# The thirteenth kernel column of a depthwise convolution as sixteen 32x32 products, two channel groups at a time

## The chip, the cores and the metric

The kernel runs on one NeuronCore of a Trainium2 chip. Its engines are TensorE (PE in the profile, with its weight loads as PEld), VectorE (DVE), ScalarE (ACT), GpSimd (POOL) and SyncE (SP). SP, ACT and POOL issue the transfers; 16 DMA engines carry them out. The metric is the time of the device in microseconds (us), as the median of three runs.

## The reference, cut to what matters

The network has four layers on an image batch x of shape (8, 384, 32, 32). Layers 0 and 1 are state space blocks; the change touches only one step of their preparation work. Layers 2 and 3 are what the change is about:

```
# layer 2: one 13x13 depthwise convolution and six smaller ones, each with a
# batch norm; the kernel folds all seven into one 13x13 kernel per channel
out = bn0(dwconv(x, w_lk)) + sum(bn_j(dwconv(x, w_bj, dilation r_j)))
# layer 3: a pointwise product, then again a 13x13 depthwise convolution
x_pw = bn(einsum('bchw,oc->bohw', x, pw_w)) + x
out  = gelu(bn(dwconv(x_pw, dwk_w)) + bn(x_pw * dw1_w))
```

So there are two 13x13 depthwise convolutions over 384 channels, 8 images and 32x32 pixels, with a pointwise product (384 to 384 channels) between them. All numbers are fp32.

## The kernel before, in words

The function `network` runs the two state space layers first (`layers`, some 6,340 us of the span), then the first depthwise convolution (`conv.run`, writing x4), the pointwise product (`point.run`, writing x5), and the second depthwise convolution (writing the output). The class `Depthwise` does both convolutions.

**One group.** A group is eight channels; `N2` is 48 groups. An image tile `xp` has 128 partitions: four blocks of 32 image rows, of which block s holds the rows shifted by s columns. A weight tile `wt` holds, for each of the 8 channels, a 128 x 32 matrix for each j in 0..3 (`KP` = 4). One product of `wt[:, c, :, j]` (128 x 32) with the image at column offset 4j (128 x 256: 8 images of 32 columns) sums over all kernel rows and over the four kernel columns 4j to 4j+3. Four channels q go to the four 32-partition quarters of one PSUM tile `ps`, so a set is 16 products (L1008), and a group has two sets a. 13 columns need four steps j, and three of the 16 columns of the last step are zeros (`prepare`, L208 to L210, lays them out so). In the profile every fp32 product is two matmul instructions with a weight load each: 48 x 32 x 2 = 3,072 for one convolution, 6,144 for both.

**Filling an image tile.** `images` (L976 to L984) has POOL issue two transfers for a group; they fill one of the four blocks for each half of the channels. Then DVE makes the shifted blocks by four copies: two of 32 x 1212 elements (L999, one for each half h) and two of 64 x 1208 (L1000 and L1001). The last of these, L1001, reads blocks 2 and 3 of the second half and so follows the second L999. There are `NB` = 4 image tiles, and the images of group g + 3 are issued in the turn of group g.

**Weights.** `kernels` (L967 to L970) loads a group's weights by four transfers of 128 KB, three issued by SP and one by ACT, in pieces of 512 bytes. There are `NK` = 11 weight tiles; the first ten groups of a convolution are loaded ahead by POOL (`early`), and the weights of group g + 10 are issued in the turn of group g, which has to wait until group g - 1 has left its tile.

**Eviction.** ACT evicts a set (`ACTIVATE`, L1013, 128 x 256) into a tile `o`, of which there are four, and then issues its store (L1014, 128 KB). The first convolution stores rows of 1,024 bytes, the second pieces of 128 bytes to the output. PSUM has eight banks; four hold `ps` tiles, and four are set aside by a placeholder, `past_ps`.

**Order.** An engine works through its instructions in one order, fixed when the program is built, by the order in the code and by what is ready. An instruction that waits holds up all behind it on its engine, and a DMA issue is such an instruction: ACT's evictions, ACT's stores and ACT's weight loads are one queue. The transfers of SP and ACT signal eight semaphores in turn (101 to 105, 107, 109 and 110 in the trace), so a new one waits until the transfer that used its semaphore last has landed. The image and weight tiles lie in SBUF behind a placeholder of `PAST` = 16,100 floats per partition, where the layers' tiles are still in use at their end; the tiles of the pointwise product lie behind them.

## Time and profile before

| what | us |
|---|---|
| median of three runs (lowest, highest) | 6903.32 (6903.21, 6914.22) |
| span of the profiled execution | 6870.5 |
| what lies around the span (median less span) | 32.8 |
| first convolution: first product to last eviction's start | 6349.3 to 6521.4 |
| pointwise product: first to last matmul | 6535.2 to 6660.8 |
| second convolution: first product to last eviction's start | 6671.5 to 6866.4 |

All positions are us from the start of the span. The clock granted to TensorE is full in both convolutions (PEclk 1.00 in all but their first microseconds). A "DMA share" above 1 means that the 16 engines had on average more than one packet each under way. The column "(x..)" counts instructions; of the 128 matmul instructions of two groups one can read how many pairs of groups went by in a stretch.

### The profile page before, as it was taken

What the parts mean: (1) busy time and instruction counts of PE and PEld (TensorE: products, weight loads), DVE (VectorE), ACT (ScalarE), POOL (GpSimd) and SP (SyncE); (2) the same over time, 40 slices, a digit from 0 to 9 for tenths busy, and PEclk for the clock granted to TensorE, in tenths of its full rate; (3) what the DMA queues carried; (4) which work ended last, traced back from release to release, by engine and by line L of the source; (5) the groups of instructions that cost most, each with busy time, mean ns of one, the idle gap of its engine ahead of it and who ended that gap; (6) DMA issues with size and microseconds to landing.
All of it is one profiled execution on the core that took longest, in us unless ns stands there. A gap on an engine that the chain in (4) does not pass through costs nothing. (4 is left out here: it accounts for less than half of the span.)

```text
span 6870.5 us, 76836 instructions
## 1 busy us (share of the span) xinstructions
PE 5851.1 (85%) x22562; PEld 2082.8 (30%) x22562; DVE 5755.9 (84%) x4598; ACT 4475.3 (65%) x7478; POOL 5285.7 (77%) x2858
## 2 busy tenths in 40 slices
PE   6787787888988888888888888888898888978988
PEld 2222222222322232222222232223232222323745
DVE  3899999899888888889889898888888898791837
ACT  4777666767676776867676767767676667653222
POOL 3889888888888888888898888888888788772412
PEclk7789988999999999999999999999999989989999
DMA  4565555665656666666756566666675655754979
GB/s 130 162 175 158 154 158 151 162 182 159 182 155 165 169 170 163 161 168 170 176 157 179 161 175 165 167 165 169 161 172 160 165 162 162 173 132 123 287 213 236
DMA packets 944578, 1160.04 MB, mean 169 GB/s; under 512 B 301264, under 2 KB 537344, under 8 KB 944160
## 3 DMA queue, kind: packets, MB, share of 16 engines
q1 hardware_dynamic: 782080, 1059.11, 59.0%
q10 hardware_dynamic: 146928, 51.02, 3.1%
q0 software_dynamic: 15152, 44.99, 2.3%
q8 instruction: 183, 3.00, 0.2%
q14 instruction: 235, 1.93, 0.1%
HBM read 904.67 MB, written 199.49 MB: 161 GB/s over the span
## 5 line engine op out<-in xcount | busy, mean ns | idle before, releaser
L532 POOL TENSOR_TENSOR dbu<-B,ru 128x1024 f32<-128x1024 f32 x1536 | 3583.2, 2357 | 168.7 <-DMA B<-bc 92.3
L525 ACT ACTIVATE h<-rd,A 128x512 f32<-128x512 f32 x3072 | 2117.4, 691 | 887.4 <-DVE hc L561 521.2
L553 DVE TENSOR_TENSOR_SCAN h<-h,state,dbu 128x512 f32<-128x512 f32 x1152 | 1482.5, 1287 | 210.5 <-ACT h L525 74.6
L561 DVE TENSOR_TENSOR hc<-h,C 128x1024 f32<-128x1024 f32 x1152 | 1411.0, 1225 | 139.8 <-DMA C<-bc 22.2
L556 DVE TENSOR_TENSOR_SCAN h<-h,dbu 128x1024 f32<-128x1024 f32 x576 | 1317.9, 2288 | 221.0 <-ACT h L525 149.9
L572 POOL TENSOR_TENSOR hc<-dbu,C 128x1024 f32<-128x1024 f32 x384 | 903.1, 2352 | 702.1 <-DVE dbu L556 358.5
L583 PE MATMUL acc<-hc,fold 128*32 128x512 f32 x6144 | 1158.0, 662 | 321.6 <-DVE hc L561 239.9
L415 PE MATMUL mm<-xt,wi 128*128 128x512 f32 x2232 | 1116.9, 638 | 57.2 <-ACT delta L491 18.9
L703 PE MATMUL f<-mx,wi 128*128 128x512 f32 x1116 | 589.0, 635 | 141.7 <-ACT fh L707 99.9
L415 PEld LDWEIGHTS mm<-xt,wi 128*128 128x128 f32 x2232 | 419.9, 201 | 754.5 <-issue 435.5
L604 PE MATMUL mm<-u,wo 128*128 128x512 f32 x1152 | 589.9, 653 | 63.4 <-DMA wo<-in_l_out_dram 51.6
L716 PE MATMUL f<-fh,wo 128*128 128x512 f32 x1128 | 573.1, 625 | 73.2 <-DMA wo<-in_fc_dram 64.1
L583 PEld LDWEIGHTS acc<-hc,fold 128*32 128x32 f32 x6144 | 164.6, 112 | 1132.3 <-DVE hc L561 513.3
L553 DVE TENSOR_TENSOR_SCAN dbu<-h,state,dbu 128x512 f32<-128x512 f32 x384 | 470.5, 1267 | 15.8 <-ACT h L525 8.0
L556 DVE TENSOR_TENSOR_SCAN dbu<-h,dbu 128x1024 f32<-128x1024 f32 x192 | 438.1, 2282 | 48.1 <-ACT h L525 47.3
L439 PE MATMUL mm<-xp,taps 128*64 128x512 f32 x1536 | 408.7, 654 | 21.2 <-ACT state L569 8.1
L984 POOL DMA_DIRECT2D xp<-x x192 | 124.3, 648 | 382.1 <-PE ps L1008 182.7
L305 ACT ACT_TABLE_LOAD x289 | 370.8, 1283 | 5.9 <-PEq L1214 0.7
L1008 PE MATMUL ps<-xp,wt 128*32 128x256 f32 x6144 | 343.8, 381 | 34.7 <-ACT o L1013 21.1
L604 PEld LDWEIGHTS mm<-u,wo 128*128 128x128 f32 x1152 | 229.8, 208 | 427.1 <-issue 355.6
L580 PE MATMUL acc<-u,skip 128*128 128x512 f32 x384 | 226.1, 673 | 153.2 <-DVE u L588 150.6
L425 ACT ACTIVATE xp<-mm,b_in 64x512 f32<-64x512 f32 x384 | 261.6, 681 | 143.1 <-PE mm L415 140.3
(168 smaller groups left out, 5726.4 us busy)
## 6 DMA issues: line engine op xcount, KB each, us to landing
ru<-uu SPq DMA_DIRECT2D x1536, 128.0 KB
rd<-dd SPq DMA_DIRECT2D x1536, 128.0 KB
wi<-w_in SPq DMA_DIRECT2D x372, 192.0 KB
xp<-xp SPq DMA_DIRECT2D x384, 128.5 KB
dd<-delta SPq DMA_DIRECT2D x192, 256.0 KB
uu<-delta SPq DMA_DIRECT2D x192, 256.0 KB
wo<-in_l_out_dram SPq DMA_DIRECT2D x96, 384.0 KB
wi<-fc_w SPq DMA_DIRECT2D x192, 192.0 KB
```

The costliest lines, as they stand in the source:

```text
L415: nc.tensor.matmul(s.ps[m], w[:, c], s.xt[:, c], start=c == 0, stop=c == KC - 1)
L439: nc.tensor.matmul(s.ps[d][64 * h : 64 * h + 64], taps[:, h, j], xp[h][:, 2 * j : 2 * j + T], start=j == 0, stop=j == 1,)
L525: nc.scalar.activation(y[:, q], s.dr[d][1][h][:, q], AF.Exp, scale=s.layer.A[:, at : at + 1])
L532: nc.gpsimd.tensor_tensor(dbu, s.B[g].unsqueeze(1).to_broadcast([P, 2, T]), s.ur[d][1][h], ALU.mult)
L553: nc.vector.tensor_tensor_scan(to[:, q], y[:, q], dbu[:, q], first, ALU.mult, ALU.add)
L556: nc.vector.tensor_tensor_scan(flat_to, flat_y, flat_b, first, ALU.mult, ALU.add)
L561: nc.vector.tensor_tensor(hc, to, s.C[g].unsqueeze(1).to_broadcast([P, 2, T]), ALU.mult)
L572: nc.gpsimd.tensor_tensor(hc, y, s.C[g].unsqueeze(1).to_broadcast([P, 2, T]), ALU.mult)
L583: nc.tensor.matmul(s.acc[d][32 * r : 32 * r + 32], k["fold"], tiles[r // 2][:, r % 2], start=False, stop=n == PER - 2)
L604: nc.tensor.matmul(s.ps[m], w[:, d], s.us[d], start=d == 0, stop=d == KD - 1)
L703: nc.tensor.matmul(s.ps[m], s.w["in", m][:, c], s.xt[:, c], start=c == 0, stop=c == KC - 1)
L716: nc.tensor.matmul(s.down, s.w["out", 2 * m + f // KD][:, f % KD], s.hs[f], start=f == 0, stop=f == KF - 1)
```

## The change

1. **Products.** Groups are taken in pairs, so a turn has four sets. Each set does only three steps j (12 columns of the kernel) with 128-row products. The 13th column is done at the end of the turn: for set k (0 to 3) its four products use only the 32 rows of block k, placed at rows 32k and columns 32q of the array. These are 16 products of 32 x 32 into four PSUM banks. `prepare` now puts the 13th column into all four blocks of the weight tile, with two DVE copies for each block in place of one.
2. **Copies.** The four copies of a group become a function `shifts`. Its last one (the old L1001) is done by ACT. It is called for the next pair, after this pair's products and ahead of this pair's evictions.
3. **Buffers.** Eight PSUM banks in place of four, six image tiles in place of four with images issued four or five groups ahead, nine groups of weights loaded early in place of ten.
4. **Memory.** The pools of the pointwise product are opened first, so that they lie in front; `PAST` falls to 3,200 floats, and `past_ps` goes.

```
-                n = (KS - s + 3) // 4
-                nc.vector.tensor_copy(rows[:, s, low : low + KS, 0:n], t[:, s::4].rearrange("p j r -> p r j"))
+                part = rows[:, s, low : low + KS]
+                nc.vector.tensor_copy(part[:, :, 0 : KP - 1], t[:, s : KS - 1 : 4].rearrange("p j r -> p r j"))
+                nc.vector.tensor_copy(part[:, :, KP - 1 :], t[:, KS - 1 :].rearrange("p j r -> p r j"))
...
-    NB, AHEAD = 4, 3
-    NK, EARLY = 11, 10
+    NB, AHEAD = 6, 4
+    NK, EARLY = 11, 9
...
+    def shifts(self, g):
+        nc, n, xp = self.nc, B * WIDE, self.xps[g % self.NB]
+        for h in range(2):
+            low, q = 2 * HW * h, slice(4 * h, 4 * h + 4)
+            nc.vector.tensor_copy(xp[low + HW : low + 2 * HW, q, 0 : n - 1], xp[low : low + HW, q, 1:n])
+        nc.vector.tensor_copy(xp[2 * HW :, 0:4, 0 : n - 2], xp[: 2 * HW, 0:4, 2:n])
+        nc.scalar.copy(xp[: 2 * HW, 4:8, 2:n], xp[2 * HW :, 4:8, 0 : n - 2])
...
+        for g in range(2):
+            self.shifts(g)
+        for pair in range(0, self.N2, 2):
+            sets = [(g, a) for g in (pair, pair + 1) for a in range(2)]
+            for g in (pair + self.AHEAD, pair + self.AHEAD + 1):
+                if g < self.N2:
+                    self.images(g, src)
+            for g in (pair + self.EARLY, pair + self.EARLY + 1):
+                if g < self.N2:
+                    self.kernels(g, table, (nc.sync, nc.scalar, nc.sync, nc.sync))
+            tops = []
+            for g, a in sets:
...
+                for j in range(KP - 1):
+                    x = columns(g, 0, P, 4 * j)
                     for q in range(4):
...
+            for k, (g, a) in enumerate(sets):
+                low, high = HW * k, HW * (k + 1)
+                x, wt = columns(g, low, high, KS - 1 - k), self.wts[g % self.NK]
+                for q in range(4):
+                    nc.tensor.matmul(
+                        tops[k][HW * q : HW * (q + 1), : B * HW], wt[low:high, 4 * a + q, :, KP - 1],
+                        x[:, 4 * a + q, :, 0:HW], start=False, stop=True, tile_position=(low, HW * q),
+                    )
+            for g in (pair + 2, pair + 3):
+                if g < self.N2:
+                    self.shifts(g)
+            for (g, a), ps in zip(sets, tops):
                 o = self.work.tile([P, B, HW], F32, tag="o", name="o")
                 nc.scalar.activation(o, ps[:, : B * HW], func, bias=bias[:, 2 * g + a : 2 * g + a + 1])
                 nc.scalar.dma_start(store(2 * g + a), o)
...
+        point = Pointwise(tc, st)
         past = st.enter_context(tc.tile_pool(name="past", bufs=1, reuse_waits="tile"))
         past.tile([P, PAST], F32, name="past")
-        past_ps = st.enter_context(tc.tile_pool(name="past_ps", bufs=1, space=PSUM, reuse_waits="tile"))
-        past_ps.tile([P, 4 * T], F32, name="past_ps")
         conv = Depthwise(tc, st)
         conv.early(got["k2"])
-        point = Pointwise(tc, st, conv.psum, a["pw"])
+        point.fill(conv.psum, a["pw"])
```

## The prediction

> **What bounds the kernel now.** I first read the busy times by stretch, to see who is full in the two convolutions.
>
> ```profile
> core 0: us, PE busy (x) PEld busy (x) DVE busy (x) ACT busy (x) POOL busy (x), PEclk, DMA share, GB/s
> 6349.00:6400.00 51.00, 50.68 (x940) 42.09 (x944) 49.02 (x61) 12.75 (x27) 16.82 (x29) 1.00 1.00 266
> 6400.00:6520.00 120.00, 117.07 (x2140) 83.71 (x2132) 104.88 (x131) 31.79 (x68) 48.25 (x75) 1.00 1.06 289
> ...
> 6700.00:6840.00 140.00, 122.40 (x2132) 79.70 (x2128) 105.83 (x135) 31.74 (x67) 45.22 (x67) 1.00 1.13 246
> ```
>
> A pair of groups is 128 matmul instructions, so a pair takes 51 x 128/940 = 6.95 us at the start of the first convolution, 120 x 128/2140 = 7.18 us in its rest, and 140 x 128/2132 = 8.40 us in the second. PE looks full, and DVE is close. But the DMA share is 1.06 and 1.13: a pair moves 16 transfers (8 of weights, 4 of images, 4 stores), and the engines that carry them never rest. Next, what PE's own speed would be: single starts in the trace come four within 39 ns, and the next four 216 ns later, so 128 instructions are 32 x 0.216 = 6.91 us. Only the first stretch runs at that. What holds the rest up is in the waits (total us, times, longest) of 6360 to 6520:
>
> ```profile
> ACT o L1013 <- PE ps L1008: 45.4, 28, 3.3
> ACT o L1013 <- DMA x<-o: 34.0, 30, 2.6
> ACT o L1013 <- DMA wt<-k_rows: 32.2, 21, 2.5
> ```
>
> and in the chain that ended last, from 6300 on:
>
> ```profile
> by line: DMA wt<-k_rows 22.8%; PE ps L1042 22.0%; DMA x<-o 9.2%; DMA out_dram<-o 9.0%; PE ps L1008 5.9%; issue 4.0%; ACTq L970 3.8%; ACTq L1014 3.8%; ACT o L1013 3.1%; PE f L716 2.8%; DVE xp L999 2.2%; DMA wo<-in_fc_dram 2.0%; DMA xt<-x 1.6
> ```
>
> The pointwise product (L1042) is bound by PE. In the convolutions the chain runs through transfers of some 5 us each and through ACT's issues; their products (L1008) are only 5.9%. A late eviction is mostly an ACT that stood before a DMA issue whose semaphore was not yet free. The weights show it too: early in the first convolution they are issued some 40 us ahead of their products, for group 40 only 9 us. So **the transfers, served through ACT's one queue, bound both convolutions** from about 6400 on.
>
> **Part by part.** *Products.* Each set loses one of four steps: per pair 12 steps of 2 x 0.216 = 5.18 us remain. The 16 small products (32 instructions) have no row. If all run abreast they cost one step, 0.43; if only the four columns run abreast, as now, 4 x 0.43 = 1.73; if one after another, 32 x 0.216 = 6.91. The trace does show what a change of shape costs: 522 ns from a 128x128 product of 512 columns to one of another shape, 429 between equal ones, so 0.09 us twice per pair. I take the first: 5.18 + 0.43 + 0.19 = 5.8 us, 1.1 us less per pair. Under a pace of 7.18 and 8.40 set by others this gain is not on the path, save at the start of a convolution.
>
> [...]
>
> *Copies.* DVE drops from four to three copies a group, 3 x 0.80 = 2.4 us for 3.2, no longer close to any bound. ACT gains one of 1208 elements per group. Its price from ACT rows:
>
> ```profile
> L456 ACT ACTIVATE zs<-zs 128x512 f32<-128x512 f32 x192 | 109.8, 619 | 0.7
> L569 ACT COPY state<-h 128x2 f32<-128x2 f32 x576 | 92.0, 160 | 331.6 <-DVE hc L561 324.2 <-DVE den L639 4.2
> L1013 ACT ACTIVATE o<-ps,b 128x256 f32<-128x256 f32 x192 | 91.0, 474 | 312.7 <-PE ps L1008 144.6 <-DMA wt<-k_rows 67.5 <-DMA x<-o 35.8
> L636 ACT ACTIVATE lg<-lg,top 8x1024 f32<-8x1024 f32 x8 | 9.2, 1148 | 0.2
> L151 ACT COPY b<-mm 128x96 f32<-128x96 f32 x2 | 0.5, 239 | 0.8 <-PE mm L150 0.8
> ```
>
> From 2 to 96 elements a copy grows by 0.84 ns each, so 0.160 + 1206 x 0.84 = 1.17 us; from 512 to 1024 the slope is 1.03, giving 1.34. I take 1.2, the copy's own rows: 2.4 us per pair.
>
> *ACT's queue.* Now ACT's own time per pair of the first convolution is 4 x 0.474 evicting, 4 x 0.36 and 2 x 0.37 issuing (median 0.33), some 0.2 between: 4.3 us. The DMA waits above are 66.2 us in 160 us, 22.3 pairs: 3.0 us each. With the copies its own time is 6.7 us. **The waits are the open price**: a landing that ACT awaits goes on while it copies, so up to 2.4 us could be absorbed; but the two weight issues now stand behind four stores in a burst, the eighth transfer before the second of them is one of these stores, and the copies and the next pair's evictions stand behind it. Waits all gone: the pace stays at the transfers' 7.18. All kept: 9.7. I take half, 6.7 + 1.5 = 8.2: +1.0 us for 24 pairs, **+24 us** (0 to +60).
>
> In the second convolution ACT's weight issue itself blocks, because the stores before it are 1,024 pieces of 128 bytes:
>
> ```profile
> L970 ACTq DMA_DIRECT2D wt<-k_rows x31: 1392/2099/3273, 6702.0 to 6829.3; - x31
> ```
>
> (min/median/max ns; 0.33 us in the first convolution.) Own time 1.9 + 4 x 0.41 + 2 x 0.33 + 0.2 + 2.4 = 6.8 us, and 2 x 1.77 = 3.5 of blocking. Half kept is 8.55: +0.15 for the 16.7 pairs of 6700 to 6840, and +1.2 for four pairs before, which ran at some 7.4: **+7 us**. All kept, 10.3: 1.9 x 16.7 + 2.9 x 4 = +43. None: 0.
>
> [...]
>
> *Ends.* A pair's four evictions now come together after its last product, where one was left: 3 x (0.47 + 0.36 + 0.1) = 2.8 us later at the end of each convolution, **+5.6 us** (0 to 7, if the last weights land earlier). *Start of a convolution.* Faster products pull stores forward while the DMA share is still 0.96 in 6671 to 6700: **-2 us** (-5 to 0).
>
> *Buffers.* Nine early weight groups with 11 tiles mean two groups loaded in the first turn in place of one: the same 11, the same bytes. The images one turn earlier move no byte less. Eight banks let PE run a pair further ahead of ACT; with ACT the slower, that fills up and then gives nothing (0). *Preparation.* 24 DVE copies of 128x39 and 128x52 (175 and 242 ns) become 24 of 39 and 24 of 13 elements: +1.4 us if the new ones cost as little as 60 ns (the smallest DVE row, a memset of one element), +3.8 at 160; DVE is 84% busy there, so I take **+2**. *Memory.* 12,768 floats of the pointwise pools plus 3,200 are 15,968, about the old 16,100, so the convolution's tiles come free as now. But three POOL memsets (1.6 us each) and SP's load of `pw` now wait for the layers' end; queued ahead of POOL's first image issue (6330.2), they would hold it until some 6347 + 4.8, and PE would start 9 us later; behind it, nothing. **+2** (0 to +9).
>
> *Sum* on the profile: 24 + 7 + 5.6 - 2 + 2 + 2 = 38.6; 6870.5 + 38.6 = 6909. With the 32.8 us between the span and the median: **6942 us**. With all waits gone, 0 + 0 + 5.6 - 2 + 2 + 0 gives 6909; with all kept and the late start 60 + 43 + 5.6 + 4 + 9 gives 7025.
>
> **Rivals.** *A, the transfers absorb it.* ACT's waits shrink as its work grows and the DMA share stays above 1: some +5 us, 6908. For it: the waits are for landings, which an occupied ACT need not see. Against: the burst of four stores.
>
> *B, faster.* The DMA engines are not at their limit, and a shorter PE turn pulls more through: the pace falls to ACT's own time, 6.7 us in the first convolution (-0.45 x 24 = -11) and 7.1 with a little blocking in the second (-1.3 x 20 = -26), with +5 at the ends: 6871. For it: within 6355 to 6357, single slices moved up to 386 GB/s. Against: 120 us at 289 with a share of 1.06. It decides once the stretches after 6400 move over some 300 GB/s, that is, a pair under 6.9 us.
>
> *C, the small products do not overlap.* PE needs 12.3 us a pair: (12.3 - 7.18) x 24 + (12.3 - 8.40) x 24 = +217, 7120. Four abreast would be 7.1 us, hidden under ACT. *The change does not do what it says* if ACT's copies end up behind the evictions in its order: then the shifts of the next pair come late, and PE waits where ACT does; this lies within the first case.
>
> **Chances.** ACT's queue 0.52, A 0.32, B 0.12, C 0.04. The range is 6888 to 7005: it leaves out most of B below, and above C and the all-kept end. A measurement of this kernel can tell about 0.2%, 14 us, from no change: same is 6889 to 6917, most of A and the small end of the first case, 0.33; faster 0.12; slower 0.55.
>
> **What would show it.** Right: an ACT copy near 1.2 us, starts of 16 small products close together, pairs of 8 us or more in the first convolution, a DMA share below 1, evictions waiting for weights and stores, PE idle on ACT. Wrong: pairs at or under 7 us with over 300 GB/s (B), an unchanged pace with a share above 1 (A), or small products 216 ns apart (C).

## The result and the profile after

The changed kernel takes 6991.98 us (median of four runs, 6984.93 to 6993.20) against 6906.62 us for the kernel before on the same chip: a ratio of 1.0122 with a 95% interval of 1.0107 to 1.0136, or +85 us. The forecast had the direction and the engine; its +39 us is less than half of what came.

One run of the kernel before was profiled again; its execution took 6905.11 us and its span was 6903.3, so 1.8 us lie around a span. The changed kernel's profiled execution took 6992.25 us with a span of 6990.5. These two are compared, and the first profile of before (span 6870.5) is given beside them. A convolution is counted from its first product to its last eviction's start, and the pointwise product from its first matmul's start to its last one's start:

| us | before, first profile | before again | changed |
|---|---|---|---|
| layers' last product starts | 6346.2 | 6375.3 | 6371.2 |
| from there to the first convolution's first product | 3.1 | 3.1 | 13.5 |
| first convolution, first product to last eviction's start | 172.0 | 169.6 | 208.0 |
| pointwise product | 125.0 | 124.7 | 125.9 |
| second convolution, as the first | 194.9 | 201.6 | 240.6 |

So of the 87 us between the spans, 38.4 lie in the first convolution, 39.0 in the second and 10.4 ahead of the first; what else differs cancels to below 1 us. The pairs' paces (from the starts of the products) went from 7.13 to 8.89 us in the middle of the first convolution (12 pairs from the seventh on) and from 8.96 to 10.68 in that of the second (15 pairs from the sixth on). The busy times by stretch of the changed kernel, with the columns shown in the prediction:

```profile
6440.00:6580.00 140.00, 121.29 (x2103) 68.16 (x2107) 75.41 (x96) 69.26 (x103) 47.37 (x69) 0.90 1.05 249
6780.00:6960.00 180.00, 131.45 (x2148) 69.61 (x2140) 77.79 (x101) 64.87 (x100) 39.69 (x67) 0.84 1.03 202
```

2148 instructions in 180 us are 10.7 us a pair. TensorE is no longer full (131.45 us of 180) and its granted clock is 0.84 where it was 1.00; VectorE fell from three quarters of the time to under half; ScalarE is busy 36%. The DMA share is still above 1, but the bytes fell from 246 to 202 GB/s (234 in the second profile of before). By busy time nobody looks full. But this busy time leaves out the issuing of transfers. The groups of instructions show that the pieces were priced about rightly, and whom the products wait for. The first line is from before_again, the others from the changed kernel:

```profile
L1008 PE MATMUL ps<-xp,wt 128*32 128x256 f32 x6144 | 343.7, 381 | 40.2 <-ACT o L1013 26.2
```

```profile
L1018 PE MATMUL ps<-xp,wt 128*32 128x256 f32 x4608 | 306.6, 420 | 108.4 <-ACT xp L988 83.9 <-DVE xp L987 23.7 <-issue 0.5
L988 ACT COPY xp<-xp 64x1208 f32<-64x1208 f32 x96 | 110.8, 1196 | 246.4 <-DVE xp L986 85.2 <-DMA xp<-x 43.8 <-DMA x<-o 39.9
```

The copy takes 1.196 us, and of the 108.4 us in which TensorE stood before a 128-row product, 83.9 ended with that copy. Before, ScalarE's lateness reached TensorE only through PSUM banks that were not yet evicted (26.2 of 40.2 us). The waits of 6440 to 6580, and then of 6780 to 6960, give the first hint of why the copy is late:

```profile
ACT xp L988 <- DMA x<-o: 39.9, 9, 8.0
```

```profile
PE ps L1018 <- ACT xp L988: 48.5, 12, 7.4
ACT xp L988 <- DMA out_dram<-o: 36.3, 5, 8.4
```

The copy itself needs no store. What the view names as the end of its idle time is a store's landing, because weight issues stand ahead of the copy in ScalarE's queue, and an issue waits until its semaphore is free: 25 of the 28 weight issues of 6440 to 6580 start within 0.04 us of the landing of the transfer that signalled the same semaphore last. In the second convolution the issues themselves are also long, those of the stores more than those of the weights (6780 to 6960; min/median/max ns):

```profile
L965 ACTq DMA_DIRECT2D wt<-k_rows x33: 357/955/3127, 6787.8 to 6958.3; - x33
```

```profile
L1036 ACTq DMA_DIRECT2D out_dram<-o x68: 401/547/5226, 6779.8 to 6957.6; - x68
```

Added up over the stretch, the 33 weight issues take 42.8 us and the 68 store issues 71.6. ScalarE's timeline has them ahead of a pair's two copies, and TensorE's has the wait:

```profile
6847.56 4.21 ACTq L1036 DMA_DIRECT2D out_dram<-o  x2
6851.81 3.63 ACTq L965 DMA_DIRECT2D wt<-k_rows  x2
6855.54 2.29 ACT L988 COPY xp<-xp 64x1208 f32<-64x1208 f32 x2 [7.64 <-DMA out_dram<-o]
```

```profile
6856.79 5.49 PE L1018 MATMUL ps<-xp,wt 128*32 128x256 f32 x72 [5.66 <-ACT xp L988]
```

In each of the 17 pairs of this stretch the first copy starts 0.10 us after the second weight issue ends, whatever landing the view names. With its issues ScalarE's queue is occupied for 168 of the 180 us, so it is nearly full though ScalarE is busy only 36%.

And the chain that ended last, from 6300 on, now runs through the queue, the copy and the images:

```profile
by line: PE ps L1067 18.3%; DMA wt<-k_rows 11.5%; issue 10.2%; DMA x<-o 8.9%; PE ps L1018 8.1%; ACTq L1036 7.3%; DMA xp<-x 4.8%; ACT xp L988 4.4%; ACTq L965 3.6%; ACT o L1035 3.1%; PE f L717 2.5%; POOL xp L979 2.4%; PE f L704 1.8%; DMA wo<-
```

The chain's share of waiting for a weight transfer's landing halved (22.8% to 11.5%); ACTq (the issues of L1036 and L965) and the copy (L988) hold 15.3%, where ACTq (L970 and L1014) held 7.6% before.

### The profile page after: what moved, and what is told of

It is laid out like the page before. It is cut to its first block, busy times and chain, and to the rows that moved or that the text cites. A ratio compares the mean times of both kernels' runs of the same rounds, so it can differ in the third digit from the quotient of the medians.

```text
span 6990.5 us, 77003 instructions
## 1 busy us (share of the span) xinstructions
PE 5883.6 (84%) x22562; PEld 2045.0 (29%) x22562; DVE 5674.4 (81%) x4526; ACT 4577.7 (65%) x7574; POOL 5288.8 (76%) x2852
## 5 line engine op out<-in xcount | busy, mean ns | idle before, releaser
L533 POOL TENSOR_TENSOR dbu<-B,ru 128x1024 f32<-128x1024 f32 x1536 | 3585.1, 2360 | 172.0 <-DMA B<-bc 88.2
L1018 PE MATMUL ps<-xp,wt 128*32 128x256 f32 x4608 | 306.6, 420 | 108.4 <-ACT xp L988 83.9
L704 PEld LDWEIGHTS f<-mx,wi 128*128 128x128 f32 x1116 | 204.6, 197 | 485.1 <-issue 261.6
```

Of the source, the lines that this page charges most:

```text
L533: nc.gpsimd.tensor_tensor(dbu, s.B[g].unsqueeze(1).to_broadcast([P, 2, T]), s.ur[d][1][h], ALU.mult)
L704: nc.tensor.matmul(s.ps[m], s.w["in", m][:, c], s.xt[:, c], start=c == 0, stop=c == KC - 1)
```

## The experiments

All runs, with the ratio to the kernel before on the same chip, and the gap ahead of the first convolution and the two convolutions of each profile (us). Two profiles of the unchanged kernel differ by 2.4 us in the first convolution and 6.7 in the second: smaller differences are not read.

| run | ratio (95%) | gap | first | second |
|---|---|---|---|---|
| before_again | | 3.1 | 169.6 | 201.6 |
| changed | 1.0122 (1.0107 to 1.0136) | 13.5 | 208.0 | 240.6 |
| after_copy_on_dve | 1.0102 (1.0079 to 1.0125) | 12.5 | 203.5 | 224.7 |
| after_weights_on_sp | 1.0151 (1.0126 to 1.0175) | 9.4 | 235.9 | 237.9 |
| before_copy_on_act | 1.0071 (1.0051 to 1.0091) | 3.1 | 184.7 | 239.7 |
| before_three_steps | 1.0011 (0.9996 to 1.0027) | 3.1 | 182.1 | 203.2 |
| copy_on_dve_8_o | 1.0102 (1.0082 to 1.0121) | 13.1 | 196.8 | 221.8 |
| pairs_four_steps | 1.0055 (1.0039 to 1.0071) | 13.8 | 192.3 | 206.7 |
| after_fill_later | 1.0126 (1.0109 to 1.0143) | 3.1 | 210.2 | 243.0 |
| before_weights_on_pool | 0.9998 (0.9988 to 1.0009) | 3.1 | 174.8 | 191.0 |
| copy_on_act_weights_on_pool | 1.0045 (1.0029 to 1.0061) | 3.1 | 196.7 | 202.6 |
| after_mended | 1.0063 (1.0048 to 1.0077) | 3.1 | 194.8 | 216.7 |
| before_half_weights | 0.9943 (0.9927 to 0.9958) | 3.1 | 167.7 | 170.0 |
| after_products_together | 1.0160 (1.0144 to 1.0175) | 12.2 | 208.9 | 249.8 |
| mended_together | 1.0060 (1.0045 to 1.0075) | 3.1 | 195.2 | 213.3 |
| small_first | 1.0074 (1.0057 to 1.0091) | 0.5 | 199.9 | 213.3 |
| small_first_half_weights | 0.9968 (0.9956 to 0.9981) | 0.5 | 170.0 | 172.6 |
| before_weights_by_pairs | 1.0009 (0.9998 to 1.0021) | 3.1 | 175.8 | 198.1 |
| before_pool_in_second | 0.9985 (0.9974 to 0.9995) | 3.1 | 171.8 | 195.4 |

**Is it the transfers, and not TensorE, that bound the kernel before?** Two runs on it, one with a quarter of the products left out, one with half of the weights' bytes.

```
# before_three_steps
-                for j in range(KP):
+                for j in range(KP - 1):
...
-                            start=j == 0, stop=j == KP - 1,
+                            start=j == 0, stop=j == KP - 2,
# before_half_weights
-            windows = bass.AP(table.tensor, at, [[KP, HW], [4 * HK * KP, 8], [1, HW * KP]])
-            queue.dma_start(wt[HW * s : HW * (s + 1)].rearrange("p q r j -> p q (r j)"), windows)
+            windows = bass.AP(table.tensor, at, [[KP, HW], [4 * HK * KP, 8 if g <= self.EARLY else 4], [1, HW * KP]])
+            queue.dma_start(wt[HW * s : HW * (s + 1), 0 : 8 if g <= self.EARLY else 4].rearrange("p q r j -> p q (r j)"), windows)
```

> The kernel before with the fourth step of every set left out, so the 13th kernel column is missing from the result and TensorE has a quarter less work in the convolutions (5.2 us a pair). Theory T (the transfers, served through ScalarE's queue, bound both convolutions of the kernel before): the first stretch, which ran at TensorE's 6.91, falls to VectorE's 6.5 at most, the rest stays near 7.18 and 8.40; within 15 us of the kernel before. Rival P (TensorE bounds them): a pair falls to VectorE's 6.5 us in both, up to 16 + 45 us faster.

> The kernel before, whose weight transfers from group 11 on carry only the first four of the eight channels (half the bytes; the other half of a tile keeps the weights of an earlier group, so the output is not the reference's). A pair's bytes fall from about 2.0 to 1.5 MB; the products, copies, evictions and the number of transfers stay. Theory T (bytes through the 16 engines set the pace): both convolutions fall to PE's own 6.91 us a pair, the first from about 170 to 166, the second from 195 to 202 to 170 to 175, and the time by 30 to 35 us to about 6870. Rival N (the number of transfers, their semaphores and the 128-byte pieces of the stores set it, not the weights' bytes): the second convolution stays above 190 and the time within 10 of before.

The first gave 6914.24 us against 6902.07, a ratio whose interval includes 1; the second 6863.90 against 6901.69, 38 us less. Two stretches of the latter:

```profile
6390.00:6530.00 140.00, 140.00 (x2601) 119.56 (x2597) 134.60 (x164) 38.48 (x81) 46.99 (x82) 1.00 0.86 235
6720.00:6860.00 140.00, 138.35 (x2568) 103.09 (x2564) 132.34 (x162) 38.01 (x80) 42.93 (x76) 1.00 1.05 223
```

140 x 128/2601 = 6.89 and 140 x 128/2568 = 6.98 us a pair: TensorE's own 6.91 in both. So the bytes bound the second convolution, by 25 to 32 us; in the first they are worth 2 to 4 us only, and with all bytes it already ran near TensorE's own pace (7.13 us). Leaving out products did not speed it up either (182.1 us), so no single bound is shown for the first.

**Is it the copy on ScalarE, or the pairs?** The copy was taken back in the changed kernel, and put alone into the kernel before:

```
# after_copy_on_dve
-        nc.scalar.copy(xp[: 2 * HW, 4:8, 2:n], xp[2 * HW :, 4:8, 0 : n - 2])
+        nc.vector.tensor_copy(xp[: 2 * HW, 4:8, 2:n], xp[2 * HW :, 4:8, 0 : n - 2])
# before_copy_on_act
-            nc.vector.tensor_copy(xp[: 2 * HW, 4:8, 2:n], xp[2 * HW :, 4:8, 0 : n - 2])
+            nc.scalar.copy(xp[: 2 * HW, 4:8, 2:n], xp[2 * HW :, 4:8, 0 : n - 2])
```

> The changed kernel with the fourth copy back on VectorE; nothing else differs. Theory Q (ScalarE's one queue sets the pace: its own 6.7 us a pair, with the two copies, and the waits before its weight issues ahead of them): ScalarE loses 2 x 1.20 us a pair, the pace falls from 8.53 to some 7.3 us a pair in the first convolution and from 10.7 to some 8.7 in the second, and the kernel gets 60 to 75 us faster than the changed one, about 6920. Rival G (grouping: what costs is that weights, images and stores now come in bursts of a pair, whoever copies): the pace stays within 0.4 us and the time above 6970.

> The kernel before with only its fourth copy moved to ScalarE. Theory Q: ScalarE has 1.20 us more per group behind its issues, and the copy is needed by the next products, so the pace rises by 0.5 to 1 us a pair, +15 to +45 us over the kernel before. Rival G: VectorE is relieved and ScalarE has room while it waits for landings; within 10 us of the kernel before.

Both have a part. The copy alone, in the kernel before, brings the whole loss of the second convolution (239.7; the changed kernel has 240.6) and 13 to 15 us of the first. Taken back, it leaves 33.9 of 38.4 us in the first and 23.1 of 39.0 in the second, so the pairs cost by themselves, and the two do not add up. The chain of before_copy_on_act, in order of time (start, us, what), shows the link:

```profile
6800.54 11.71 PE ps L1008 x160
...
6812.27 0.44 ACT o L1013
...
6813.08 0.40 ACTq L1014
...
6813.52 2.16 ACTq L970
...
6815.77 1.21 ACT xp L1001
...
6817.02 10.31 PE ps L1008 x160
```

An eviction, its store, a weight issue blocked for 2.2 us, the copy, and only then the products that read it. From 6812.24 to 6817.02 these products have no input; TensorE has one other set to do meanwhile and then stands idle for 3.10 us. It is a loop, and each link is in series. The granted clock is lower there too: 160 instructions at 216 ns for four would be 8.6 us, and took 11.7 and 10.3 at a granted clock of 0.75 and 0.86.

**Is it the blocked weight issue ahead of the copy?** The weight transfer that ScalarE issues was given to POOL, with the copy on ScalarE and in the kernel as it was:

```
-                self.kernels(g + self.EARLY, table, (nc.sync, nc.scalar, nc.sync, nc.sync))
+                self.kernels(g + self.EARLY, table, (nc.sync, nc.gpsimd, nc.sync, nc.sync))
```

> The run with only the last copy of a group on ACT (time ratio 1.0071, second convolution 239.7 us) with the weights' fourth transfer issued by POOL in place of ACT. Theory L (the loss comes from the loop eviction, store, blocked weight issue, copy, products: the issue stands ahead of PE's input): the second convolution falls from 239.7 to about 205 or less, and the time to within 0.2% of the kernel before. Rival W (it is the copy's own 1.2 us a group on a full ACT, 2.4 us a pair): the second convolution stays above 225 and the time at or above 1.005 times that of before. Half way, 210 to 225, both have a part.

> The kernel before with one edit: the one weight transfer of each group that ACT issued (L996 of before) is issued by POOL. Theory L (it is the weight issue on ACT that costs, blocked for 1.4 to 3.3 us behind the stores of the second convolution, 2.1 in the median): the second convolution, 195 to 202 us from first product to last eviction, loses up to 2 x 1.8 us a pair less what the transfers take in its place, so 175 to 190; the first is unchanged; the time falls by 10 to 25 us, to about 6880. Rival T (the transfers themselves set the pace and it does not matter who issues them): both convolutions and the time as before, 6900, within 7. Rival R (POOL becomes late with the images, which wait behind the weight issue): the first convolution above 180 us and the time above 6910.

With the copy on ScalarE the second convolution fell from 239.7 to 202.6, as the theory of the blocked issue has it. Its stretch of 6740 to 6900, before the edit and after it:

```profile
6740.00:6900.00 160.00, 121.25 (x1868) 72.97 (x1864) 71.14 (x91) 61.74 (x88) 37.03 (x59) 0.85 0.96 207
```

```profile
6740.00:6900.00 160.00, 135.57 (x2368) 89.15 (x2364) 88.42 (x113) 79.62 (x112) 74.21 (x111) 1.00 1.14 255
```

2368 instructions in place of 1868, 255 GB/s in place of 207, and the clock is back at 1.00, with the copy still on ScalarE. So in the second convolution of the kernel before with this one edit, the loss came from the blocked issue ahead of the copy. The copy is not free even so. The first convolution rose by 12 us (184.7 to 196.7), and its trace shows a shorter loop that is left (ScalarE's timeline, then TensorE's):

```profile
6465.60 0.48 ACT L1013 ACTIVATE o<-ps,b 128x256 f32<-128x256 f32 x1 [1.58 <-PE ps L1008]
6466.10 0.33 ACTq L1014 DMA_DIRECT2D x<-o  x1
6466.52 1.20 ACT L1001 COPY xp<-xp 64x1208 f32<-64x1208 f32 x1 [0.45 <-ACT o L1013]
```

```profile
6463.56 3.69 PE L1008 MATMUL ps<-xp,wt 128*32 128x256 f32 x64 [0.52 <-ACT xp L1001]
6467.77 3.69 PE L1008 MATMUL ps<-xp,wt 128*32 128x256 f32 x64 [0.52 <-ACT xp L1001]
```

A set is done, ScalarE evicts it, issues its store and makes the copy for the next group, and that group's second set starts: 4.21 us a group, 8.42 a pair, with nothing blocked and at a granted clock of 1.00. Most pairs of the first convolution take just this, and most of the second 8.52. That is more than the 7.13 of the kernel before in the first, so the copy costs time there by its place behind the eviction; and it is less than the 8.96 in the second, so nothing is lost there. The built order decides it: here the copy of a group stands behind both evictions of the group before from the sixth group to the forty-fourth, and in before_copy_on_act only in every sixth group of the first convolution. So the time came down to 1.0045 only, not to that of the kernel before. In the kernel as it was the same edit gave no measurable difference.

Giving the transfer to SP in the changed kernel:

```
-                    self.kernels(g, table, (nc.sync, nc.scalar, nc.sync, nc.sync))
+                    self.kernels(g, table, (nc.sync, nc.sync, nc.sync, nc.sync))
```

> The changed kernel with all four weight transfers of a group issued by SyncE, none by ScalarE; the copy stays on ScalarE. Theory Q in the form that the blocked weight issue ahead of the copies is what costs (the profile has weight issues, copies and evictions in this order on ScalarE, and TensorE waits for the copy): ScalarE's own time is 6.0 us a pair and it waits for stores no more, so the pace falls to some 7.2 in the first convolution and 8.6 in the second, 6915 to 6930. If the copy's 1.20 us themselves are what costs: a gain of under 20 us. Rival G: within 10 us of 6992.

It was no gain: 1.0151, with the first convolution at 235.9 in place of 208.0 and the second at 237.9 in place of 240.6. The theory had forecast 6915 to 6930, so in the changed kernel the weight issue on ScalarE is not all that holds it. The trace of 6790 to 6950 shows what took its place: TensorE stood only 10.7 us for the copy (48.5 in the changed kernel's 6780 to 6960), but 16.6 us for weights, VectorE stood 56.1 us for images, and ScalarE's store issues still took up to 3.9 us each. A changed kernel with the copy on ScalarE and this transfer on POOL was not run.

**What do the pairs cost?** First, whether evictions wait for output tiles (eight `o` tiles in place of four, copy on VectorE), and whether it is the burst of four evictions at a pair's end (the 13th column as a fourth step of 128 rows, each set evicted as it is done, copy on VectorE, and the old `prepare`):

```
# copy_on_dve_8_o: after_copy_on_dve, and
-        self.work = st.enter_context(tc.tile_pool(name="d_work", bufs=4, reuse_waits="tile"))
+        self.work = st.enter_context(tc.tile_pool(name="d_work", bufs=8, reuse_waits="tile"))
# pairs_four_steps: after_copy_on_dve, and (the loop of small products goes)
-                for j in range(KP - 1):
+                for j in range(KP):
...
-                            start=j == 0, stop=False,
+                            start=j == 0, stop=j == KP - 1,
```

> The changed kernel with the fourth copy on VectorE, and eight o tiles in place of four. In the run with the copy on VectorE the evictions waited 73 us for stores in 130 us of the first convolution (27 times) and TensorE then waited for evictions. Theory O (the four evictions of a pair wait for their o tiles, whose stores of the pair before have not landed): these waits go, the pace falls from 8.26 to some 7.4 us a pair and from 10.1 to some 8.7, 35 us faster than 6974. Theory S (the waits are those of the DMA issues between the evictions, whose semaphores are still held by other transfers; the profile puts them down to the same stores): the pace stays within 0.3 us, within 10 us of 6974.

> The changed kernel with the copy on VectorE, and with the 13th column done as before, in a fourth full step of each set, so that a set can be evicted as soon as it is done; loads still in pairs. TensorE has 6.9 us a pair again in place of 5.8. Theory E (the four evictions and stores that come together at the end of a pair are what grouping costs): the pace falls to that of the kernel before, 7.2 and 8.5, some 40 us faster than 6974 though TensorE has more to do. Rival L (the weights and images asked for in pairs are what costs): it stays near 8.3 and 10.1, 6965 to 6985.

Twice the output tiles changed nothing in the time (1.0102 both). The four-step pairs are 32 us quicker than after_copy_on_dve, with TensorE doing more. Their stretches of 6760 to 6920, after_copy_on_dve and then pairs_four_steps:

```profile
6760.00:6920.00 160.00, 118.11 (x2088) 68.30 (x2084) 112.31 (x144) 26.93 (x64) 47.93 (x67) 0.85 1.06 213
```

```profile
6760.00:6920.00 160.00, 133.45 (x2288) 90.38 (x2284) 123.84 (x158) 34.14 (x72) 51.07 (x70) 0.98 1.12 231
```

A pair has 128 instructions in both: 9.8 us and 9.0. This points to the burst: in the first run's waits of 6440 to 6570 ScalarE's evictions stood 73.4 us behind landings of stores, and TensorE 24.8 us behind evictions. It is no proof, since TensorE's clock rose too, and the small products went with it.

**The images ahead of the first convolution.** The clears of the pointwise tiles and their weights were issued after the first convolution:

```
-        point.fill(conv.psum, a["pw"])
         conv.run(
...
         )
+        point.fill(conv.psum, a["pw"])
```

> The changed kernel with the pointwise product's weights and cleared tiles asked for after the first convolution's code in place of ahead of it. Theory M (the three clears of 1.6 us on GpSimd, which wait for the layers' last product, hold up the first images by 45 us and the first product by some 10): the gap between the layers' last product and the first product of the convolution falls from 13.5 us to some 3 to 5, and the kernel gets about 9 us faster, 6983. If the images were late for another reason, the gap stays.

POOL's timeline in the changed kernel, at the layers' end:

```profile
6369.39 1.62 POOL L1056 MEMSET q_out<- 128x1824 f32 x1 [68.86 <-PE f L717]
6371.96 3.17 POOL L1056 MEMSET q_out<- 128x1824 f32 x2 [0.95 <-PE f L717]
6375.09 4.35 POOL L979 DMA_DIRECT2D xp<-x  x8
```

The images are issued after three clears that wait for the layers' last products. Moved, the gap fell from 13.5 to 3.1 us as expected, but the time did not: 6992.97. In its profile the layers ended at 6386, 15 us later than in the changed kernel, and their last `wo` load took 8.5 us beside the images. The layers' end lies between 6346 and 6390 in the profiles of all kernels, so whether the 10 us were given back there or lost in that spread is open. That spread is also why the pieces of the time are read from the convolutions and not from the spans.

**All three mended.** The edits of after_copy_on_dve, copy_on_act_weights_on_pool and after_fill_later together:

> The changed kernel with three edits: the fourth copy of a group back on DVE, the fourth weight transfer issued by POOL, and the pointwise tiles' clears and weights issued after the first convolution. If the three measured losses (the copy on ACT, the blocked issue on ACT, 10 us of late images) add up, 85 less 17 less 10 less some 25 in the second convolution leaves about 33: 6935. If the grouping by itself (four evictions and stores together at a pair's end) is what is left, it does not fall below 6915. If the shorter products are worth anything once the queue is clear, it falls below 6900.

6943.71 us, 1.0063: half of the loss is gone, half stays. Its trace showed a thing that I had not looked for: the order in which the products were built is not that of the code. TensorE's timeline of the changed kernel:

```profile
6449.00 0.73 PE L1026 MATMUL ps<-xp,wt 32*32 32x256 f32 x24
6449.66 1.53 PE L1018 MATMUL ps<-xp,wt 128*32 128x256 f32 x24
6451.12 0.66 PE L1026 MATMUL ps<-xp,wt 32*32 32x256 f32 x8
6451.72 4.12 PE L1018 MATMUL ps<-xp,wt 128*32 128x256 f32 x72
6455.77 0.73 PE L1026 MATMUL ps<-xp,wt 32*32 32x256 f32 x24
```

After a pair's last 24 small ones come the next pair's first set, its own 8 small ones, the other three sets (72), and their 24. From start to start a pair is 0.66 + 1.46 + 0.60 + 4.05 = 6.77 us. In the mended kernel they are in four stretches, and its 2.07 us a stretch make 8.27 a pair. That is the bound of its first convolution: from the fourth pair on nearly every pair takes 8.27 us there, and TensorE is busy without a pause (6400 to 6560):

```profile
6400.00:6560.00 160.00, 160.00 (x2512) 82.31 (x2498) 133.43 (x167) 37.88 (x80) 91.62 (x118) 1.00 1.09 266
```

Two runs hold TensorE to the order of the code and change nothing else:

```
+        with tc.manual_schedule(engines={mybir.EngineType.PE}):
             conv.run(...)
```

> The changed kernel with PE's order in the two convolutions held to the order of the code. In the changed kernel as it was built, the sixteen small products stand together in only 13 of 48 pairs; in the others they stand in two stretches, twelve and four, with 128-row products between, and the trace has a pair at 4.05 + 0.66 + 1.46 + 0.60 = 6.77 us of PE's own time where the run with the copy on DVE, whose sixteen stand together, has 5.35 + 0.69 = 6.04. Nothing else is edited. Theory Q (ACT's queue sets the changed kernel's pace of 8.4 to 10.7 us, PE stands on it): within 10 us of the changed kernel, 6980 to 7000. Rival S (the split costs on the path, since after each wait for ACT the pair's PE time follows in series): 0.73 us for some 35 pairs, 25 us, so 6965 or below.

> The mended kernel (copy on DVE, fourth weight transfer on POOL, pointwise clears later; 6943.7) with PE's order held to that of the code. As built its small products stood in four stretches a pair, each stretch of 24 matmul instructions with its small ones 2.03 to 2.09 us: 8.27 us a pair, which is the pace of its first convolution (8.27). Theory S (the split order is what bounds that convolution): 194.8 falls to 180 or less, the second convolution from 216.7 to about 205, the time to 6915 to 6925. Rival G (four evictions and stores in a burst bound it): both convolutions within 8 us of what they were and the time above 6930.

Neither gained: the changed kernel became rather slower (1.0160), the mended one stayed (1.0060). The split costs TensorE 0.7 us a pair in the changed kernel and 2.2 in the mended one (6.04 us when the sixteen stand together). In the changed kernel TensorE was not what was late; why that kernel became slower is open. In the mended kernel's first convolution TensorE was, yet with the order held another bound stands at the same place (195.2 us in place of 194.8). In mended_together:

```profile
6480.14 0.79 PE L1026 MATMUL ps<-xp,wt 32*32 32x256 f32 x32
6480.89 1.53 PE L1018 MATMUL ps<-xp,wt 128*32 128x256 f32 x24
6485.41 5.81 PE L1018 MATMUL ps<-xp,wt 128*32 128x256 f32 x72 [2.98 <-ACT o L1035]
6491.15 0.78 PE L1026 MATMUL ps<-xp,wt 32*32 32x256 f32 x32
```

The time that the order gives back is lost again in waiting for a PSUM bank that ScalarE has not evicted.

**Small products first.** They open the sums, the four sets follow, and each set is evicted as it is done, so the burst is gone too:

```
+            for k, (g, a) in enumerate(sets):
...
+                        x[:, 4 * a + q, :, 0:HW], start=True, stop=False, tile_position=(low, HW * q),
...
+            for (g, a), ps in zip(sets, tops):
...
+                            start=False, stop=j == KP - 2,
...
+                nc.scalar.activation(o, ps[:, : B * HW], func, bias=bias[:, 2 * g + a : 2 * g + a + 1])
+                nc.scalar.dma_start(store(2 * g + a), o)
```

> The change rearranged: the sixteen small products of a pair come first (they open the sums), the four sets of 128-row products follow, and each set is evicted and stored as soon as it is done; the copies all on DVE, the weights as in the change, the pointwise clears after the first convolution, PE's order as written. If the copy on ACT, the burst at a pair's end, the split of the small products and the late images are the whole loss, the first convolution is back at 170 to 176 and the second at 195 to 205: 6895 to 6910. If loading two groups' weights and images at one time costs by itself, as the 20 us of the first convolution in the four-step run suggest, the first stays near 190 and the time above 6920. A gain of more than 15 us over the kernel before would need the transfers to be no bound, against the run with half the weights.

> The same, with weight transfers from group 11 on that carry four of the eight channels (half the bytes; the output is not the reference's). The kernel before with half the weights ran at PE's own 6.91 us a pair, 167.7 and 170.0 us, 6863.9. Theory T (transfers bound both; with fewer bytes the shorter products show): the pace falls to the 6.04 us of 128-row and small products together, both convolutions to about 150, the time to 6825 to 6835. Rival: the order of evictions and weight issues on ACT still holds it, the convolutions at or above 165 and the time at 6860 or more.

At 6947.15 us the first is no better than the mended kernels, though its burst is gone; so the burst is not all that is left. (Its fourth weight transfer is issued by ScalarE again.) With half of the weights' bytes TensorE's timeline shows what the rearranged change can do, and what its start costs:

```profile
6379.68 0.66 PE L1017 MATMUL ps<-xp,wt 32*32 32x256 f32 x8
6383.86 1.08 PE L1017 MATMUL ps<-xp,wt 32*32 32x256 f32 x8 [3.52 <-DVE xp L988]
6385.53 1.86 PE L1017 MATMUL ps<-xp,wt 32*32 32x256 f32 x16 [0.60 <-issue]
6387.32 8.22 PE L1026 MATMUL ps<-xp,wt 128*32 128x256 f32 x96
6395.48 0.84 PE L1017 MATMUL ps<-xp,wt 32*32 32x256 f32 x32
6396.24 5.42 PE L1026 MATMUL ps<-xp,wt 128*32 128x256 f32 x96
6401.59 0.95 PE L1017 MATMUL ps<-xp,wt 32*32 32x256 f32 x32
6402.47 5.42 PE L1026 MATMUL ps<-xp,wt 128*32 128x256 f32 x96
```

From the second pair on a pair is 5.35 + 0.88 = 6.23 us, 0.7 less than TensorE's 6.91 before. But the first pair ends 15.8 us after its first product, since both groups must be copied before its small products can go (3.52 us on VectorE's last copy), and its large ones ran at a low clock (0.74 granted in 6380 to 6400). Its ratio is 0.9968 where the kernel before with half the weights has 0.9943 (the intervals just overlap, at 0.9956 to 0.9958). So the shorter products show only where fewer bytes move, and even there the whole is not quicker than the kernel before with the same bytes.

**What else is in the pairs?** The weights of two groups issued at once, alone, in the kernel before:

```
-    NK, EARLY = 11, 10
+    NK, EARLY = 11, 9
...
-            if g + self.EARLY < self.N2:
-                self.kernels(g + self.EARLY, table, (nc.sync, nc.scalar, nc.sync, nc.sync))
+            for e in (g + self.EARLY, g + self.EARLY + 1) if g % 2 == 0 else ():
+                if e < self.N2:
+                    self.kernels(e, table, (nc.sync, nc.scalar, nc.sync, nc.sync))
```

> The kernel before, but the weights of two groups are issued together in every second turn (nine groups early, as in the change); products, copies, evictions, images and the four-step sums stay as they were. Theory B (what is left of the loss in the mended kernels is the grouping of the transfers: eight weight transfers at once through SP's and ACT's shared eight semaphores, then a gap): the first convolution rises from about 170 to 180 or more, the second by 5 or more, the time to 6910 to 6925. Rival E (it is the burst of evictions and stores and the start, where two groups have to be ready before the first pair, and not the weights): both convolutions within 5 us of before, the time within 10.

1.0009, with an interval that includes 1: the grouping of the weights by itself is at most a small part of it. **Open**: how the rest of the pairs' loss (in after_mended, mended_together and small_first 23 to 30 us in the first convolution and 12 to 22 in the second) divides among the burst, the start, the images by twos and the copies of a pair at once.

**A version against both.** The fourth weight transfer on POOL in the second convolution alone, where its issue on ScalarE was blocked:

```
-                self.kernels(g + self.EARLY, table, (nc.sync, nc.scalar, nc.sync, nc.sync))
+                self.kernels(g + self.EARLY, table, (nc.sync, nc.gpsimd if func == AF.Gelu else nc.scalar, nc.sync, nc.sync))
```

> The kernel before with the fourth weight transfer issued by POOL in the second convolution alone. With it in both, the second convolution fell to 191.0 and the first rose to 174.8, and the time was the same (0.9998). If the two effects are each their own, the first stays at 170 to 172 and the second is 190 to 192: 6 to 10 us less, a ratio of about 0.9988. If the fall in the second was no more than the spread between executions (194.9 and 201.6 in the two profiles of before), the ratio is 1.000 within 0.001.

6891.70 us against 6907.30, 0.9985 with an interval that excludes 1: quicker than both kernels, by some 10 us over the kernel before, a small gain, and one of seventeen edits that were run. The second convolution of its one profile (195.4) lies between those of before (194.9 and 201.6), so the place of the gain is not shown.

## Why the prediction was right and wrong

*The bound.* Right for the second convolution: without a quarter of the products nothing was gained, with half the weights TensorE's pace came back. For the first the bytes were worth 2 to 4 us only and fewer products gained nothing either; "both" was too much.

*Products.* Nearly right, and off the path as said. No row of before stood behind the choice of 0.43, the smallest of the three estimates. The sixteen together take 0.69 us to the next product (0.43 and 0.19 for two changes of shape were forecast), and the others 5.35 (5.18): 6.04 for 5.8, in after_copy_on_dve, where they stand together. That the built order splits them in the changed kernel (6.77) the prediction did not see; holding the order gained nothing there.

*The copy's price.* 1.2 forecast, 1.196 measured.

*ACT's queue, second convolution: the step that failed.* The engine was right; the term was sized wrongly. The prediction took half of the 3.5 us of blocking a pair as kept, 8.55 us a pair and +7 us in all. It came to +39, at 10.68 us a pair; "all kept" had given 10.3. The half came from the thought that landings go on while ScalarE copies, and no row stood behind it: in the second convolution (6700 to 6840) of the first profile ScalarE's work and issues already filled 126 of 140 us. That the stores' pieces of 128 bytes are what blocks a weight issue was not shown either, since no run changed them; the trace shows the length (2.1 us in the median there, 0.33 in the first convolution), and that SyncE's issues of the same weights took 0.30 us in the median in the changed kernel's 6780 to 6960, where ScalarE's took 0.96. What the runs showed in place of the half: the blocking was not halved, it moved. The weight issues of a pair fell from 4.1 to 2.6 us, but its four store issues, priced at 0.41 each, rose from 2.5 to 4.3. And the copy is TensorE's input and stands behind these issues, so the blocking is in a loop through TensorE, where before it only delayed outputs, with four banks of slack. before_copy_on_act alone reproduces the length (239.7), and moving the weight issue takes it away there (202.6). The prediction had even written that the copies "stand behind" the weight issues, and priced it as ScalarE's sum in place of following who waits for the copy. In the changed kernel itself the copy's share is not so cleanly shown: with the copy back on VectorE 23.1 of the 39.0 us remain, and with the weight issue on SP nearly all.

*ACT's queue, first convolution.* +24 forecast, +38 measured, inside its bounds (0 to +60); here the term mixes two causes. The copy alone makes 13 to 15; with the copy taken back 33.9 remain, so the two do not add up.

*Pairs, the term put at nearly nothing.* The prediction counted the grouping only at the ends and gave the buffers 0. With the copy back on VectorE the pairs by themselves leave 33.9 and 23.1 us. Of what they consist is only in part shown.

*Ends and start.* From the last product's start to the last eviction's start, the second convolution's end rose from 0.45 to 2.97 us, +2.5 for the 2.8 forecast, and the first's from 0.9 (2.0 in the first profile) to 5.2, more than forecast. The start of the second convolution did not gain 2: its first five pairs ran at 10.36 us in place of 7.59.

*Preparation.* The +2 cannot be read, as the layers' end moves by up to 44 us between profiles.

*Memory.* The mechanism named (clears ahead of the images) was there; its place in the order was the bad one of the two, +10.4 us against a bound of +9. Its worth in the time is open.

*The 32.8 us around the span.* Wrong as a thing: 1.8 us lie around a span. The first profile was of an execution whose layers ended 14 us or more earlier than in every other profile. The forecast did not suffer, since span and remainder together made the median.

*The signs.* Right: the copy, the small products close together, pairs over 8 us, TensorE idle on ScalarE. Wrong: "a DMA share below 1". It stayed at 1.03 to 1.05 while the bytes fell. Wrong too: "evictions waiting for weights and stores". ScalarE stood idle 62.2 us before evictions (317.1 in before_again) and 246.4 before copies.

*Rivals.* A fell: the waits were not absorbed. B fell: the stretches shown moved 249 and 202 GB/s, not over 300. C fell: the 32 instructions of the small products took 0.69 us together, not 6.91.

## What to carry to other kernels

Before an operation moves to an idle-looking engine, ask what stands ahead of it in that engine's queue, and who waits for its result. Here the copy, an input of TensorE, stood behind blocked DMA issues and paid their wait in series: in 6780 to 6960 each pair's first copy started 0.10 us after the second weight issue, and TensorE stood 48.5 us for the copies. In the kernel before evictions, outputs, stood there, and TensorE stood 26.2 us for banks that were not evicted, in both convolutions together (before_again). Count the engine's issues with its work: ScalarE, busy 36%, had a queue occupied for 93% of the stretch. The price of the copy itself, right to 1% (1.2 us for 1.196), said nothing on that. And a saving on the busiest engine should not be counted on before a run with the other suspect relieved (half the bytes, a quarter less products) has said who is late.

## What the runs showed of the hardware

The DMA share can stay above 1 while fewer bytes move: 1.13 at 246 GB/s in the first profile of before, 1.03 at 202 GB/s in the changed kernel. It is no proof that the engines move all they can.

The granted clock was 0.84 in 6780 to 6960 of the changed kernel, where TensorE paused for up to 7.4 us, and a 128-row matmul instruction took 434 ns on average there, 382 in 6700 to 6840 of the first profile of before at 1.00; in copy_on_act_weights_on_pool, with pauses of up to 1.2 us before the copy (6760 to 6900), it was 1.00. That the pauses lower the clock, and how much of the loss is the clock, was not tried by itself. With a quarter of the products left out, the first convolution took 182.1 us, more than with all of them (169.6), at a clock of 0.95 in its middle.

A stretch of 32x32 products cost 0.60 us to the next large product with 8 instructions (changed kernel), 0.66 with 24 (there) and 0.69 with 32 (after_copy_on_dve): four times the instructions added 0.09 us. What the rest of the price is was not tried apart.

A store issue occupied ScalarE's queue for 0.33 to 1.37 us in 6440 to 6580 of the changed kernel (0.34 in the median), in its first convolution, and for 0.40 to 5.23 us in 6780 to 6960 (0.55 in the median), in its second.
